# Masked attention over a sparse graph: q rows fetched two tiles ahead, attention started one stage earlier, two loads of W_v issued one stage earlier

## The chip, the cores and the metric

The kernel runs on one core of one Trainium2 chip. The metric is the device time of one execution in microseconds (us). The time before is the median of three runs, 630.4 us (630.32 to 631.99). All arithmetic is in 32-bit floats.

## The reference

One transformer-like layer on a graph of 2708 nodes with 1024 features. `adj` is a 0/1 matrix with about four ones in a row (probability 0.0014771 an entry), so that only a few scores of a row count; the rest is masked with -10000.

```python
h = relu(layernorm(x))                       # x: (2708, 1024)
q, k, v = h @ W_q.T + b_q, h @ W_k.T + b_k, h @ W_v.T + b_v
z = (q @ k.T) / 32                           # scale 1/sqrt(1024)
z = where(z * adj == 0, -10000, z * adj)
x = x + relu(softmax(z, axis=1) @ v)
```

## The kernel before, in words

**What is multiplied.** The kernel first forms M = W_q^T W_k on TensorE, so that a row of "q" is h M plus a bias and a score is the dot product of such a row with a row of h. Nobody forms k. Nor is v formed for all nodes: the weighted sums u of rows of h are multiplied with W_v at the end. Nodes are sorted by their number of neighbours and put into 21 full tiles of 128 rows and one small rest; tile t of a half has at most K[t] neighbours in a row: K = 8, 7, 5, 5, 4, 3, 3, 2 for tiles 0 to 7 and 8, 7, 6, 6, 5, 5, 4, 4, 3, 3, 3, 2, 1 for tiles 8 to 20. Entry 21 (`SECOND`) holds the neighbours over eight of the tiles 0 and 8, seven of them. Tile 20 (`BARE`) has no scores to compute.

**Units and stages.** The main loop (line 1233) goes over 20 units. Units 0 to 9 form q for a pair of tiles: (0, 1), (2, 3) up to (18, 19). Units 10 to 19 multiply the sums u of a pair of tiles with W_v, in the pairs of the list `order` (line 989): (6, 5), (4, 3), (2, 0), (20, 7), (17, 13), (18, 12), (19, 11), (15, 10), (14, 1), (16, 9); tile 8 is left over and done alone at the end. "Stage n" is the pass of the loop for unit n. A unit is a product of two 256-row-by-1024 blocks by Strassen's scheme in its Winograd form: seven products of half-size blocks instead of eight. Each product is one call of `add_block`: four matmul calls, which the profile counts as eight matmuls. `multiply` (line 1046) issues for unit n in this order: s2 T1, a12 B21, s4 B22, s3 T2, then by `between` and `opened` the first two products of unit n+1 (a11 B11, and s1 with T0 in a q unit or with `M[:, 0, 1]` in an o unit), and last a22 T3. B11, B12, B21 and B22 are the quarters of the right-hand matrix: `M[:, 0, 0]`, `M[:, 0, 1]`, `M[:, 1, 0]`, `M[:, 1, 1]`; T0 to T3 are differences of them, in `T[:, 0]` to `T[:, 3]` (the same memory as `wlow`). Between those products `after(i)`, i from 0 to 6, emits everything else: "slot (n, i)" is the i-th of stage n.

**The left-hand operands.** They are needed transposed. In a q unit the rows (`qr`) are gathered from `h_dram` by GpSimd (line 1209, issued in stage n for unit n+2) and TensorE transposes them (line 415). In an o unit the rows of a tile t are either "faced" or held. A faced tile's u is copied in quarters by ScalarE (line 944), stored to `u_dram` (line 946) and loaded by four DMAs of SyncE's queue (line 700), after which VectorE can finish the transposition (line 705). A held tile's u stays in SBUF and TensorE transposes it. `sums` decides when a tile's last sum is emitted (line 940): faced if that is in slot 2 of the stage two before its unit or earlier, or if the unit is the last. s1 to s4 are then formed on VectorE (line 722 and 742).

**Attention.** `attention` (line 959) is a generator that is drained in between: for each tile it emits K[t] score steps on VectorE (line 863: one pass over a gathered tile `g` of h rows and the tile `pq` of q rows, summed up into `zall`), the softmax weights (lines 904 to 912, exponential on ScalarE), and K[t] - 1 weighted sums on VectorE (line 923; line 929 for tiles 0 and 8). The rows of h are gathered by GpSimd into eleven slots `g` (line 610), as slots come free; from stage 10 on two more slots lie in the memory of T0. `fetch(t)` asks for a tile's gathers and gets its q rows: by an indirect gather from `q_dram` for tiles under 8 (line 835, `pq<-q_dram,tab`), by a plain DMA on GpSimd's queue from `q_late` for the others (line 833). The tiles `pq` have a tag with two buffers. Tile t+1 is fetched when tile t's scores have been emitted. Each q unit stores its q rows by SyncE's or ScalarE's queue (line 1086) in `c12` or `c21`.

**What sets the order.** VectorE executes in the order in which the program emits (`manual_schedule`), so a step that waits holds up all that was emitted behind it. How many attention steps are emitted in a slot is planned: a score or a sum counts 1.3, the weights 0.6, and `advance(share)` (line 999) emits steps until the slot's share is used up; `share` (line 1241) is 20.9/7, less 2.3/7 for each faced tile of the next unit, and a little different in stages 9, 10 and the last five. Before, `advance` is first called in slot (5, 0). Where a tile must be ready and isn't (lines 1313 and 1332), steps are emitted beyond the share. SyncE's queue takes its DMAs one after the other: a DMA that waits for a semaphore holds up those behind it.

**W_v.** The four quarters of W_v replace those of M at the change from q to o units (stages 7 to 10; `last_q` is 9). Lines 1268 to 1271 load them on SyncE's queue: W_v's B11 into `M[:, 0, 1]` in stage 7, where it becomes the difference B12 - B11, then in slot (9, 0) B22 into `T[:, 0]` and B11 into `M[:, 0, 0]`, and in slot (9, 3) B21. VectorE forms T1, T2 and T3 from them at slots (9, 3), (10, 0) and (10, 1) (line 1282), and ScalarE copies B22 to its place in slot (9, 4) (line 1274). The last products of a q unit that read `M[:, 0, 0]` and `T[:, 0]` are the two that `opened(9)` issues in stage 8; the first that reads W_v's B11 is that of `opened(10)` in stage 9.

**The end.** The lone tile 8 has its own last products (lines 1382 to 1392): its rows are transposed by VectorE into `T_alone` (line 1329) and TensorE takes them after the last s3 T2.

Of the kernel before, what the change touches and what calls it, by code (L numbers as in the profile page):

```python
# [29 lines left out]
EARLY = 8  # L30
BARE = 20
# [34 lines left out]
def tile_preln_masked_attention(  # L66
# [12 lines left out]
    nc = tc.nc  # L79
# [14 lines left out]
    SECOND = NT - 1  # L94
# [81 lines left out]
    t = 0  # L176
    while t < NT:
# [4 lines left out]
        t = e  # L182
# [17 lines left out]
    M = core.tile([P, 2, 2, 4, NB], FT, name="M")  # L200
# [232 lines left out]
    T = wlow.rearrange("p (k a) (b w) -> p k (a b) w", a=2, b=2)  # L433
# [12 lines left out]
    with tc.tile_pool(name="w", bufs=1, side="left") as wp:  # L446
# [4 lines left out]
        for o in range(DC):  # L451
            nc.sync.dma_start(wq_sb[o], wq_rows[o * P:(o + 1) * P, :])
            part = slice(0, NB) if o == 0 else slice(0, D)
# [4 lines left out]
        t1 = [work.tile([P, D], FT, tag="hT", name=f"t1_{k}", bufs=2) for k in range(2)]  # L458
# [40 lines left out]
        part = stat.tile([P, 3], FT, tag="part", name="part", bufs=1)  # L499
# [107 lines left out]
    def gather(dst, src, t, w, n, skip=False):  # L607
        off = bass.IndirectOffsetOnAxis(ap=ptab.bitcast(U32)[:n, t, w:w + 1], axis=0)
        if skip:
            return nc.gpsimd.indirect_dma_start(out=dst, out_offset=None, in_=src, in_offset=off,  # L610
                                                bounds_check=N - 1, oob_is_err=False)
        return nc.gpsimd.indirect_dma_start(out=dst, out_offset=None, in_=src, in_offset=off)

    rows_of = {}
    FIRST = EARLY // 2
# [187 lines left out]
    wanted, g_of, tq, first_q = [], {}, {}, []  # L803
# [11 lines left out]
    def ask(t):  # L815

        g_of[t] = []
        wanted.extend((t, s) for s in range(K[t]))

    def fetch(t):  # L820

        if t not in g_of:
            ask(t)
        if t == BARE:
            return
        assert formed.issuperset(range(EARLY) if t < EARLY or t == SECOND else (t,)), t
        tq[t] = work.tile([P, D], FT, tag="hT", name=f"pq_{t}", bufs=2)
        if t == SECOND:
            assert EARLY in formed
            gather(tq[t][:HP], q_dram[:, :], t, SLOTS - WIDE, HP)  # L830
            nc.gpsimd.dma_start(tq[t][HP:], q_late[:HP, :])
        elif t >= EARLY:
            nc.gpsimd.dma_start(tq[t], q_late[(t - EARLY) * P:(t - EARLY + 1) * P, :])
        else:
            got = gather(tq[t], q_dram[:, :], t, SLOTS, P)
            if t == order[0]:
                first_q.append(got)

    def fill():
        while wanted and free:  # L840
            t, s = wanted.pop(0)
            g = free.pop(0)
            if s == K[t]:
                half = slice(HOSTS.index(t) * HP, (HOSTS.index(t) + 1) * HP)
                nc.gpsimd.dma_start(g[:HP], v_dram[half, :])
            else:
                with tc.issue_after(first_q[0].ins) if first_q else nullcontext():
                    gathered.append(gather(g, h_dram[:, :], t, s, P, skip=True))
            g_of[t].append(g)

    def chained(step):

        with tc.issue_after(chain[-1].ins):
            chain.append(step())

    def scores(t, then):
        k = K[t]
        for s in range(k if t != BARE else 0):  # L860
            fill()
            junk = work.tile([P, D], mybir.dt.uint8, tag="junk", name="junk2", bufs=1)
            chained(lambda: nc.vector.scalar_tensor_tensor(  # L863
                junk, g_of[t][s], 1.0, tq[t], op0=ALU.mult, op1=ALU.mult, accum_out=zall[:, t, s:s + 1]))
            yield 1.3
        tq.pop(t, None)
        if then is not None:
            fetch(then)
        fill()
        w = stat.tile([P, SLOTS + 1], FT, tag="w", name=f"w_{t}")  # L870
        if t not in EMPTY:
            nc.scalar.activation(w[:, :k], zall[:, t, 0:k], AF.Exp)
        ws[t] = w
# [79 lines left out]
    def marked(lo, hi):  # L953

        with tc.issue_after(chain[-1].ins):
            nc.vector.tensor_scalar(valid[:, lo:hi], ptab.bitcast(U32)[:, lo:hi, 0:SLOTS], float(N) - 0.5, NONE,
                                    op0=ALU.is_lt, op1=ALU.max)

    def attention(order):
        for t in order[:2]:  # L960
            ask(t)
        free.extend(slots)

        fetch(order[0])
        fill()
        yield 0.0
        marked(0, EARLY)
        yield 0.0
        after = order[1:] + [None, None]
        yield from scores(order[0], after[0])  # L970
        for i, t in enumerate(order):
            nxt = after[i]
            ahead = nxt is not None and K[t] + K[nxt] <= HIGH + 1
            part = scores(nxt, after[i + 1]) if nxt is not None else iter(())
            if ahead:

                for _ in range(min(2, K[nxt] - 1)):
                    yield next(part, 0.0)
            weights(t)
            yield 0.6  # L980
            if ahead:
                yield from part
            yield from sums(t)
            yield from part

    done, held, ws, us = set(), {}, {}, {}
    formed = set()
    faced_tiles, whole_second = set(), []
    order = [6, 5, 4, 3, 2, 0, 20, 7, 17, 13, 18, 12, 19, 11, 15, 10, 14, 1, 16, 9, 8]
    assert sorted(order) == list(range(FULL))  # L990
    chain = placed
    stream = attention(order[:order.index(0)] + [SECOND] + order[order.index(0):])
# [6 lines left out]
    def advance(us):  # L999

        spent[0] -= us
        while spent[0] < 0:
            step = next(stream, None)
            if step is None:
                break
            spent[0] += step

    def add_block(bank, a, b, last=True):
        for c in range(4):
            mm = nc.tensor.matmul(bank, a[:, c, :], b[:, c, :], start=False, stop=(c == 3), skip_group_check=True)  # L1010
        return mm
# [3 lines left out]
    def opened(n):  # L1015

        if n not in banks_of:
            return
        X, Z = banks_of[n]
        ops = ops_of[n][0]  # L1020
        add_block(X, ops["a11"], M[:, 0, 0])
        Y = psum.tile([P, NB], FT, tag="acc", name="psy")
        nc.scalar.copy(Y, X)
        if n == FIRST:
            follow("o0")
        products.append(add_block(Z, ops["s1"], T[:, 0] if units[n][0] == "q" else M[:, 0, 1]))
        p5 = small("p5")
        nc.scalar.copy(p5, Z)
        opened_of[n] = Y, p5

    def between(n):

        if n == len(units) - 1:
            single["first"] = one_started(single["banks"], single["turned"][:, 0:4, :])
        else:
            opened(n + 1)

    def one_started(banks, a):

# [150 lines left out]
    def of_wv(i, j):  # L1190

        return wv[j][:, i * 4:(i + 1) * 4, :]
# [26 lines left out]
    last_q = len(q_pairs) - 1  # L1219
# [13 lines left out]
    for n, unit in enumerate(units):  # L1233
# [7 lines left out]
        share = (20.9 if n < len(units) - 5 else 21.5) / 7  # L1241
        if n in (last_q, last_q + 1):
            share -= 2.3 / 7 * (n - last_q + 1)
        nxt = units[n + 1] if n + 1 < len(units) else None
# [4 lines left out]
        def after(i):  # L1249
# [15 lines left out]
                    with tc.issue_after(sorted_at[-1].ins):  # L1265
                        nc.vector.memset(g, 0.0)
            b11, t1, b21, b22 = M[:, 0, 0], M[:, 0, 1], M[:, 1, 0], M[:, 1, 1]
            for at, place, src in (((-2, 0), t1, of_wv(0, 0)), ((0, 0), T[:, 0], of_wv(1, 1)), ((0, 0), b11, of_wv(0, 0)),
                                   ((0, 3), b21, of_wv(1, 0))):
                if (n - last_q, i) == at:  # L1270
                    nc.sync.dma_start(place, src)
            if (n - last_q, i) == (0, 4):
# [21 lines left out]
                nc.vector.tensor_scalar(msq, msq, MLIMIT, None, op0=ALU.is_gt)  # L1294
            if n > FIRST:
                advance(share)
            if nxt is not None:

                if i == (3 if n == 0 else 4 if turn else 0):
                    ops_of[n + 1] = blocks(*rows_of[n + 1], nc.gpsimd if n + 1 < FIRST - 1 else None)  # L1300
                    with tc.issue_after(products[-1].ins) if n + 1 == FIRST else nullcontext():
                        ops_of[n + 1][1]()
                if i == (4 if n == 0 else 5 if turn else 2):
                    ops_of[n + 1][2]()
                    rows_of.pop(n + 1)
                    if n == last_q - 1:
                        all_rows()
                if i == 3:
                    banks_of[n + 1] = banks_for(bp_sb)
                if i == 6 and n + 2 < FIRST:  # L1310
                    natural_rows(n + 2)
                if i == (2 if FIRST <= n <= last_q - 2 else 3 if n == last_q else 4) and n + 2 > FIRST and n + 2 < len(units) and n + 2 not in rows_of:
                    while units[n + 2][0] == "o" and not done.issuperset(units[n + 2][1:]):
                        advance(1.0)
                    rows_of[n + 2] = load_rows(units[n + 2])
# [259 lines left out]
```

## Time and profile before

| what | us |
|---|---|
| median of three timed runs | 630.4 |
| profiled execution, its own time | 635.63 |
| span of the profiled execution, first to last instruction | 633.9 |
| TensorE busy (1579 matmuls) | 623.0 (98%) |
| VectorE busy | 525.2 (83%) |
| GpSimd busy | 370.7 (58%) |
| ScalarE busy | 291.6 (46%) |
| chain that ended last, share on TensorE | 96% |
| mean granted TensorE clock | 0.994 |

In the profile PE is TensorE's matmuls, PEld its weight loads, DVE VectorE, ACT ScalarE, POOL GpSimd and SP SyncE; "SPq" and "POOLq" are the queues of their sequencers. A line of the timeline gives the start and the duration in us, the engine, the line of the kernel, the operation, the tiles it writes and reads (`out<-in`, buffer numbers left out), the number of merged instructions, and in brackets the idle time of the engine before it with what ended it. `ps`, `psy` are the banks of a unit's products, `a`, `s` its left-hand operands, `M` and `wlow` the right-hand ones, `pt` a bank for transposes, `qr` rows for a q unit, `or` rows for an o unit, `pq` q rows of attention, `g` rows of h.

### The profile page before, as it was taken

Reading aid. Unit: us, or ns where it says so; the run is one execution under the profiler, and the core shown is the slowest. Engines: PE = TensorE matmul, PEld = TensorE weight load, DVE = VectorE, ACT = ScalarE, POOL = GpSimd, SP = SyncE. Lnnn points to the kernel's source line nnn. Section 1 sums busy time; section 2 is a strip of 40 time slices with the busy share of each in tenths; the row PEclk is TensorE's granted clock in tenths of the full one; section 3 lists DMA queues with packets and bytes.
Section 4 is the critical chain, followed back from the end, with each engine's and each line's share of the span. In section 5 each row is a group of like instructions: output and inputs, shape, how many; then the busy total and the mean of one; then the engine's idle time right before and its main releaser. Section 6 shows DMA issues by size and latency. Waiting matters only on the chain.

```text
span 633.9 us, 6066 instructions
## 1 busy us (share of the span) xinstructions
PE 623.0 (98%) x1579; PEld 312.0 (49%) x1579; DVE 525.2 (83%) x1022; ACT 291.6 (46%) x421; POOL 370.7 (58%) x394
## 2 busy tenths in 40 slices
PE   9999999999998999999999989999999999999996
PEld 5777766444444544444444434444444444444442
DVE  5999879898897845899897879998988998988741
ACT  3538985749477372443332333444433324342300
POOL 2639960885766677666543432878566776762241
PEclk9999999999999999999999989999999999999999
DMA  8999997598788469996686999899999999996391
GB/s 333 407 365 316 340 351 301 207 320 307 262 257 337 135 196 369 296 410 191 207 343 197 362 346 305 261 335 318 330 285 344 291 297 307 341 286 172 102 295 71
DMA packets 65089, 182.19 MB, mean 287 GB/s; under 512 B 9960, under 2 KB 20024, under 8 KB 64409
## 3 DMA queue, kind: packets, MB, share of 16 engines
q0 software_dynamic: 26656, 86.02, 43.3%
q1 hardware_dynamic: 31594, 71.53, 32.7%
q10 hardware_dynamic: 6798, 24.20, 9.8%
q8 instruction: 14, 0.23, 0.2%
q14 instruction: 27, 0.21, 0.1%
HBM read 146.70 MB, written 43.36 MB: 300 GB/s over the span
## 4 chain that ended last, share of the span: by engine, by line
PE 96%; DMA 3%; issue 0%; POOL 0%; SPq 0%; DVE 0%; ACT 0%; POOLq 0%
PE ps L1010 44%; PE psy L1010 32%; PE ps_y L476 6%; PE ps_x L476 4%; PE ps_z L476 4%; PE pt L415 3%; DMA M<-in_wv_dram 2%; DMA qr<-h_dram,tab 1%; PE ps_y L511 1%; PE ps_h L1226 0%; PE ps_v L594 0%; DVE y_alone L1391 0%; POOL out_dram L1375 0%; ACT q L1101 0%; POOLq L1397 0%
## 5 line engine op out<-in xcount | busy, mean ns | idle before, releaser
L610 POOL DMA_INDIRECT g<-h_dram,tab x93 | 120.5, 1296 | 62.7 <-ACT u L912 21.7
L1010 PE MATMUL ps<-M,a 128*128 128x512 f32 x320 | 145.8, 599 | 2.0 <-DMA M<-in_wv_dram 2.0
L1010 PE MATMUL psy<-wlow,s 128*128 128x512 f32 x320 | 145.1, 596 | 0.0
L863 DVE SCALAR_TENSOR_TENSOR junk<-g,pq 128x1024 uint8<-128x1024 f32 x92 | 112.4, 1221 | 11.8 <-issue 4.9
L1010 PE MATMUL ps<-M,s 128*128 128x512 f32 x240 | 107.9, 592 | 0.0
L1010 PEld LDWEIGHTS ps<-M,a 128*128 128x128 f32 x320 | 60.4, 192 | 75.4 <-issue 71.2
L1010 PEld LDWEIGHTS psy<-wlow,s 128*128 128x128 f32 x320 | 60.6, 192 | 72.9 <-issue 71.9
L923 DVE SCALAR_TENSOR_TENSOR u<-g,coef,u 128x1024 f32<-128x1024 f32 x70 | 89.7, 1281 | 5.5 <-ACT u L912 4.0
L389 DVE FIND_INDEX8 at<-ones,adj 128x8 uint32<-128x685 f32 (+1 forms) x88 | 74.5, 865 | 0.0
L1010 PEld LDWEIGHTS ps<-M,s 128*128 128x128 f32 x240 | 45.5, 190 | 57.2 <-issue 56.5
L1010 PE MATMUL psy<-wlow,a 128*128 128x512 f32 x160 | 71.9, 592 | 0.0
L368 ACT ACTIVATE sized<-adj 128x2708 uint8<-128x2708 f32 (+1 forms) x22 | 54.2, 2465 | 7.9 <-DMA adj<-in_adj_dram 6.6
L1111 POOL DMA_INDIRECT y<-in_x_dram,tab x19 | 34.6, 1821 | 35.6 <-ACT y L1128 24.2
L298 POOL TENSOR_TENSOR hsum<-hsum,x 128x256 f32<-128x256 f32 (+1 forms) x56 | 38.8, 738 | 25.5 <-DVE wlow L444 21.4
L1010 PEld LDWEIGHTS psy<-wlow,a 128*128 128x128 f32 x160 | 30.4, 190 | 38.3 <-issue 37.1
L808 POOL DMA_INDIRECT out_dram<-y,tab x21 | 27.0, 1287 | 19.2 <-issue 13.1
L1010 PE MATMUL ps<-wlow,s 128*128 128x512 f32 x80 | 36.0, 593 | 0.0
L944 ACT COPY v<-u 128x1024 f32<-128x1024 f32 x19 | 19.8, 1044 | 29.1 <-DVE u L923 25.8
L760 ACT COPY ps<-bp_sb 128x512 f32<-128x512 f32 x42 | 24.6, 595 | 10.3 <-DVE y L1146 9.7
L626 POOL DMA_INDIRECT tab_dram<-tab,pos_i x22 | 21.7, 985 | 11.2 <-DVE pos_i L689 5.7
L276 ACT ACTIVATE x<-x,r 128x1024 f32<-128x1024 f32 (+1 forms) x22 | 25.8, 1232 | 5.2 <-POOL r L266 5.2
L912 ACT ACTIVATE u<-g,coef 128x1024 f32<-128x1024 f32 x16 | 18.4, 1149 | 21.3 <-DVE coef L911 13.2
(253 smaller groups left out, 843.4 us busy)
## 6 DMA issues: line engine op xcount, KB each, us to landing
adj<-in_adj_dram SPq DMA_DIRECT2D x21, 1354.0 KB
x<-in_x_dram SPq DMA_DIRECT2D x21, 512.0 KB
h_dram<-x ACTq DMA_DIRECT2D x21, 512.0 KB
u_dram<-v ACTq DMA_DIRECT2D x19, 512.0 KB
or<-u_dram SPq DMA_DIRECT2D x76, 128.0 KB
q_late<-q SPq DMA_DIRECT2D x12, 512.0 KB
pq<-q_late POOLq DMA_DIRECT2D x12, 512.0 KB
M<-in_wv_dram SPq DMA_DIRECT2D x3, 1024.0 KB
```

The lines of the kernel that those rows point to most:

```text
L276: nc.scalar.activation(xs[i][:n], xs[i][:n], AF.Relu, bias=r[:n, 4, i:i + 1], scale=r[:n, 3, i:i + 1])
L298: small.append(nc.gpsimd.tensor_add(hsum[:n, cols], hsum[:n, cols], xt[:n, cols]))
L368: nc.scalar.activation(sized[:n], a[:n, :, :PW], AF.Abs, accum_out=total[:n, t:t + 1])
L389: nc.vector.max_index(at[:n, k - first_k, g, :], ones[:n, 0:8], a[:n, g, :])
L476: mm = nc.tensor.matmul(bank, a_tile(o + H * a[0], a[1], i), b(o), start=first and o == 0, stop=(o == H - 1), skip_group_check=True)
L610: return nc.gpsimd.indirect_dma_start(out=dst, out_offset=None, in_=src, in_offset=off, bounds_check=N - 1, oob_is_err=False)
L760: nc.scalar.copy(return_[h], row[:, h * NB:(h + 1) * NB])
L808: to = nc.gpsimd.indirect_dma_start(out=out, out_offset=bass.IndirectOffsetOnAxis(ap=ptab.bitcast(U32)[:n, t, SLOTS:SLOTS + 1], axis=0), i ...
L863: chained(lambda: nc.vector.scalar_tensor_tensor(junk, g_of[t][s], 1.0, tq[t], op0=ALU.mult, op1=ALU.mult, accum_out=zall[:, t, s:s + 1]))
L923: chained(lambda: nc.vector.scalar_tensor_tensor(u, g_of[t][s], coef[:, s:s + 1], u, op0=ALU.mult, op1=ALU.add))
L1010: mm = nc.tensor.matmul(bank, a[:, c, :], b[:, c, :], start=False, stop=(c == 3), skip_group_check=True)
L1111: return nc.gpsimd.indirect_dma_start(out=y[:n], out_offset=None, in_=x, in_offset=off, compute_op=ALU.add)
```

## The change

Five things, in one edit:

- `fetch` no longer asks for a tile's gathers; that is done when the tile before it has been scored, as before. The q rows of tile t+2 (not t+1) are fetched when tile t's scores have been emitted; a tile whose q isn't formed yet is put on a list, `awaited`, and fetched at the first later score step where it is.
- The q rows of the first two tiles (6 and 5) are fetched at the start.
- `advance(2 * share)` is called in slot (4, 6), so that attention's first steps are emitted there.
- Tile 13 stands ahead of tile 17 in `order`, and so in attention and in unit 14.
- The loads of W_v's B22 (`T[:, 0]`) and B11 (`M[:, 0, 0]`) are emitted in `between` of stage 8, right behind `opened(9)`, instead of in slot (9, 0).

```diff
+    awaited = []
+
+    def is_formed(t):
+        return t == BARE or formed.issuperset(range(EARLY) if t < EARLY or t == SECOND else (t,))
+
+    def fetch_formed():
+        while awaited and is_formed(awaited[0]):
+            fetch(awaited.pop(0))
+
     def fetch(t):
-        if t not in g_of:
-            ask(t)
         if t == BARE:
             return
...
-    def scores(t, then):
+    def scores(t, then, later):
         k = K[t]
         for s in range(k if t != BARE else 0):
+            fetch_formed()
             fill()
...
         tq.pop(t, None)
-        if then is not None:
-            fetch(then)
+        if then is not None and then not in g_of:
+            ask(then)
+        if later is not None:
+            awaited.append(later)
+        fetch_formed()
         fill()
...
         fetch(order[0])
+        fetch(order[1])
         fill()
...
-    order = [6, 5, 4, 3, 2, 0, 20, 7, 17, 13, 18, 12, 19, 11, 15, 10, 14, 1, 16, 9, 8]
+    order = [6, 5, 4, 3, 2, 0, 20, 7, 13, 17, 18, 12, 19, 11, 15, 10, 14, 1, 16, 9, 8]
...
         else:
             opened(n + 1)
+        if n == last_q - 1:
+            nc.sync.dma_start(T[:, 0], of_wv(1, 1))
+            nc.sync.dma_start(M[:, 0, 0], of_wv(0, 0))
...
-            for at, place, src in (((-2, 0), t1, of_wv(0, 0)), ((0, 0), T[:, 0], of_wv(1, 1)), ((0, 0), b11, of_wv(0, 0)),
-                                   ((0, 3), b21, of_wv(1, 0))):
+            for at, place, src in (((-2, 0), t1, of_wv(0, 0)), ((0, 3), b21, of_wv(1, 0))):
...
             if n > FIRST:
                 advance(share)
+            elif (n, i) == (FIRST, 6):
+                advance(2 * share)
```

More of the change, by code (lines that the diff above doesn't have):

```diff
@@ L818, in ask @@
         wanted.extend((t, s) for s in range(K[t]))
+    awaited = []
[4 more added lines that the diff above has]
+            fetch(awaited.pop(0))
     def fetch(t):
-        if t not in g_of:
-            ask(t)
         if t == BARE:
             return
-        assert formed.issuperset(range(EARLY) if t < EARLY or t == SECOND else (t,)), t
+        assert is_formed(t), t
         tq[t] = work.tile([P, D], FT, tag="hT", name=f"pq_{t}", bufs=2)
@@ L968, in attention @@
         yield 0.0
-        after = order[1:] + [None, None]
-        yield from scores(order[0], after[0])
+        after = order[1:] + [None, None, None]
+        yield from scores(order[0], *after[:2])
         for i, t in enumerate(order):
@@ L973, in attention @@
             ahead = nxt is not None and K[t] + K[nxt] <= HIGH + 1
-            part = scores(nxt, after[i + 1]) if nxt is not None else iter(())
+            part = scores(nxt, *after[i + 1:i + 3]) if nxt is not None else iter(())
             if ahead:
```

## The prediction

> **What bounds the kernel now.** I read the page's first part, then TensorE's waits, then TensorE's timeline around those waits, then the queues that feed it.
>
> ```profile
> PE 623.0 (98%) x1579; PEld 312.0 (49%) x1579; DVE 525.2 (83%) x1022; ACT 291.6 (46%) x421; POOL 370.7 (58%) x394
> ```
>
> ```profile
> core 0 of [0], span 633.9 us
> engine line waited for: us in total, times, longest us
> PE pt L415 <- DMA qr<-h_dram,tab: 2.1, 1, 2.1
> PE ps L1010 <- DMA M<-in_wv_dram: 2.0, 1, 2.0
> ```
>
> TensorE is the bound, and in the whole span it waits for a transfer only twice. So the change can gain only by ending such a wait or by taking matmuls away, and can lose only by making TensorE wait somewhere new. The two waits in TensorE's timeline (start, duration, last bracket the idle time before):
>
> ```profile
> 202.98 1.54 PE L415 MATMUL pt<-ident,qr 128*128 128x128 f32 x8 [2.08 <-DMA qr<-h_dram,tab]
> 204.32 4.85 PE L1010 MATMUL psy<-wlow,s 128*128 128x512 f32 x8
> 209.01 1.04 PE L415 MATMUL pt<-ident,qr 128*128 128x128 f32 x8
> ```
>
> ```profile
> 347.57 3.60 PE L1010 MATMUL psy<-wlow,a 128*128 128x512 f32 x8
> ...
> 361.30 3.60 PE L1010 MATMUL psy<-wlow,s 128*128 128x512 f32 x8
> 366.93 5.37 PE L1010 MATMUL ps<-M,a 128*128 128x512 f32 x8 [2.03 <-DMA M<-in_wv_dram]
> 372.13 3.60 PE L1010 MATMUL ps<-M,s 128*128 128x512 f32 x8
> ```
>
> A block (x8, four calls of `add_block`) starts 3.43 us after the one before it: from 347.57 to 361.30 are four blocks in 13.73. At the second wait the start-to-start times are 5.63 and 5.20, so 2.20 us were waited and 1.77 us more were lost in the block behind it: 3.97 us in all. The first wait, by the same reading, cost 2.08, then 4.69 - 3.43 = 1.26 in its block and, with eight transposes at 0.87 (the row at 526.79 below), 1.34 - 0.87 = 0.47: 3.8 us. The windows view says what the extra time is (columns: stretch, its length, then busy time of PE, PEld, DVE, ACT, POOL, then the granted clock, the DMA share and GB/s):
>
> ```profile
> 366.90:372.10 5.20, 5.17 (x8) 2.21 (x9) 2.25 (x3) 0.00 (x0) 3.37 (x3) 0.67 1.03 353
> ```
>
> The clock granted behind the wait was 0.67. 5.20 x 0.67 = 3.5, the normal block: the extra is the clock, and it goes with the wait.
>
> **W_v's loads (a gain).** The wait ends with B11 (`M[:, 0, 0]`, 1 MB). The load queue of SyncE in order of time:
>
> ```profile
> 351.81 0.34 SPq L1086 DMA_DIRECT2D q_late<-q  x1
> 352.25 0.38 SPq L1271 DMA_DIRECT2D wlow<-in_wv_dram  x1
> 352.95 5.44 SPq L1271 DMA_DIRECT2D M<-in_wv_dram  x2
> ```
>
> Both loads stood behind the store of q tile 17, which waits for stage 8's last copy. Their places are free earlier: the last matmul that reads `T[:, 0]` for unit 9 is the block in front of 347.57. Issued there, the two loads leave at about 347.8 and 348.5, 4.5 us sooner. B11 would land at 366.8 - 4.5 = 362.3; TensorE wants it at 361.30 + 3.43 = 364.73. That leaves 2.4 us. Is there room on the DMA engines? What the queues moved in 347.8 to 352.3, and then in 352.3 to 366.8 (packets, MB, share of 16 engines; q1 is SyncE's, q0 GpSimd's):
>
> ```profile
> q0 software_dynamic: 364, 1.30, 89.2%
> ```
>
> ```profile
> q1 hardware_dynamic: 484, 3.05, 50.0%
> q0 software_dynamic: 711, 2.10, 40.5%
> ```
>
> In the first stretch SyncE's queue was empty and the neighbour gathers had the engines. In the second, with both full, SyncE's queue got half of them. If half is what it gets from 347.8 on, the loads keep their pace and, with q 17's 0.5 MB no longer in front, beat 362.3. If the gathers kept their 89% until 352.3, the loads would gain only the store's place: 0.5 MB at 3.05 MB in 14.5 us is 2.5 us, landing at 364.3, still before 364.73 by a hair. The first row pair is the nearer case (two full queues), so I take the whole wait as gone: -3.97. Bound on the other side: no gain, if the loads stay put. A gain above 3.97 is excluded, as no other wait hangs on these loads.
>
> TensorE wants B22's product `T[:, 1]` only at stage 10; VectorE's subtraction for it waited too (row 364.17 below) and comes earlier with T0.
>
> **Eight transposes go (a gain).** The planner charges 1.3 for a score or sum, 0.6 for weights, and hands out `share` = 20.9/7 = 2.99 a slot. `advance(2 * share)` at (4, 6) emits 5.97 worth: all three scores of tile 6 and two of tile 5, five steps that stood in slots (5, 0) and (5, 1). From there every tile's last sum falls about two slots earlier. Counting it through: tile 10's last sum moves from (15, 3) to (15, 1). Tile 10 belongs to unit 17, and `sums` turns its rows on the way through DRAM if it ends by (15, 2); otherwise TensorE transposes them. Before, these are the eight in stage 16:
>
> ```profile
> 261.79 6.87 PE ps L1010 x16
> ...
> 526.79 0.87 PE pt L415 x8
> ```
>
> After, they are gone (-0.87); tile 1 keeps its eight, its slot (16, 4) is the same. VectorE gets two half-tile transposes instead (a whole tile is 1.25 us, row 609.07 below), and a store and four loads of 0.5 MB each way are added, issued a stage ahead of their use. The profiled sum is -3.97 - 0.87 = -4.84 us.
>
> **Steps moved into stage 4 (no cost on TensorE).** VectorE runs them in program order, ahead of unit 6's sums s1 to s4:
>
> ```profile
> 247.62 1.23 DVE L863 SCALAR_TENSOR_TENSOR junk<-g,pq 128x1024 uint8<-128x1024 f32 x1 [4.71 <-issue]
> ...
> 255.02 1.28 DVE L722 TENSOR_TENSOR s<-a,pt 128x512 f32<-128x512 f32 x2 [1.79 <-ACT a L718]
> ```
>
> ```profile
> 239.96 1.04 POOL L612 DMA_INDIRECT pq<-q_dram,tab  x1 [0.30 <-issue]
> ```
>
> The 4.71 idle is tile 5's first score; its q rows were asked of GpSimd at 239.96 only, behind six neighbour gathers. Now they are second in that queue, so this idle goes, and the gathers behind start one issue (1.04 + 0.30) later. A score is 1.25 with the short read behind it (1.23 in the row), so unit 6's s1 is then at 255.0 + 5 x 1.25 - 4.71 - 1.79 + 1.34 = 256.1. TensorE takes it in the second half of the row at 261.79, at 265.2: 7.8 us of cover after the 1.28 of the operation. Were the cover gone, each us of lateness is a us of TensorE, plus the clock.
>
> **Rows of q two tiles ahead; 13 before 17.** The fetch for tile t+2 writes the buffer of tile t, so GpSimd waits for t's last score; behind it in GpSimd's queue stand t+1's neighbour gathers and the row gathers of units 7 to 9. The kernel has such waits already, at the same points:
>
> ```profile
> POOL pq L612 <- DVE junk L863: 8.9, 5, 4.4
> ```
>
> so I cost this at nothing (tile 13 ahead of 17 swaps the same operations); the rows of a unit are gathered nearly two stages (a stage is over 24 us) before use. On VectorE a wait goes: tile 17's first score.
>
> ```profile
> 364.17 2.29 DVE L1282 TENSOR_TENSOR wlow<-wlow,M 128x2048 f32<-128x2048 f32 x1 [1.71 <-DMA wlow<-in_wv_dram]
> ...
> 371.21 1.23 DVE L863 SCALAR_TENSOR_TENSOR junk<-g,pq 128x1024 uint8<-128x1024 f32 x1 [2.95 <-DMA pq<-q_late]
> ```
>
> 1.71 + 2.95 = 4.66 us of idle VectorE lie just where TensorE gains 3.97, so VectorE keeps up.
>
> **What is late next: the end.** With TensorE 4.84 us earlier, the lone last tile decides:
>
> ```profile
> 534.58 0.69 DVE L1127 TENSOR_TENSOR u<-ps,u 128x512 f32<-128x512 f32 x1 [0.57 <-PE ps L1010]
> ...
> 590.95 0.68 DVE L1127 TENSOR_TENSOR u<-ps,u 128x512 f32<-128x512 f32 x1
> ...
> 609.07 1.25 DVE L705 STREAM_TRANSPOSE T_alone<-or 128x1024 f32<-128x1024 f32 x1 [10.76 <-DMA or<-u_dram]
> ```
>
> ```profile
> 610.78 3.60 PE L1010 MATMUL ps<-M,T_alone 128*128 128x512 f32 x8
> ```
>
> Its turned rows are ready at 610.3, half a us before TensorE takes them. At 534.58 VectorE still waits for TensorE; in stage 18 it is late: the bank of 590.95 was ready eight blocks before 610.78, at 583.3. By the planner's count four sums are forced in at (16, 4) before (tile 1 was not done) and none after. A sum is
>
> ```profile
> L923 DVE SCALAR_TENSOR_TENSOR u<-g,coef,u 128x1024 f32<-128x1024 f32 x70 | 89.7, 1281 | 5.5 <-ACT u L912 4.0
> ```
>
> 1.28 us, so 5.1 us of VectorE leave this stretch, and the lone tile comes 5.1 us earlier for a TensorE that comes 4.84 earlier: the half us stays. Without this cover the end would give back up to 4.3 us.
>
> **Against the timed runs.** The profiled execution took 635.63 (span 633.9 and 1.73 around it), 5.23 over the median of 630.4. TensorE's blocks cost the same in both; only waits and the two ends can be shorter. If all 5.23 came out of the two waits' 7.8 us, 2.6 are left, and of W_v's 3.97 about 1.3; if none did, 3.97. I take the middle, 2.65, and with 0.87 the gain is 3.5: **626.9 us**, bounds 625.5 and 628.2. Under 0.3% (1.9 us) a change can't be told from none here.
>
> **Rivals.** (1) *The wait is mostly the profiler's, or the loads stay behind the store.* The order of SyncE's queue is fixed at compile time, and the trace of before can't show the new one. For it: 5.23 us must come from somewhere. Then the transposes and at most 0.9 more are gained: 628.6 to 629.5.
>
> (2) *q 17 comes late (slower).* Its store now stands behind 2 MB of W_v. The Trainium skill's "DMA: Bandwidth & Descriptors", section "Queues, rings and completion order", says the same against this change: within a ring descriptors are consumed in order, and the engines go round between the queues by packet; the half and half above agrees with the latter. By rows: B11 lands at 362.3, the store takes 7.94 as before (351.81 to the fetch that waited for it):
>
> ```profile
> 359.75 1.15 POOL L833 DMA_DIRECT2D pq<-q_late  x2 [4.02 <-DMA q_late<-q]
> ```
>
> and the fetch 11.46 (to 371.21): tile 17 could start at 381.7 at worst. Behind its first score VectorE has, up to unit 11's s1, two subtractions (2.29 each), three scores and two sums (6.3), four half-tile transposes (2.5) and s1 (0.64): 14.0. TensorE wants s1 seven blocks after 372.13, at 396.1 - 4.0 = 392.1. So it decides from 378.1 on; at 381.7 it costs 3.6 and 1.8 of clock: 626.9 + 5.4 = 632.3. Against it: the store's 7.94 and the fetch's 11.46 were measured beside W_v, which would be over by then.
>
> (3) *The slow block is not the wait's.* The Trainium skill's "TensorE: Matmul & The Clock Gate", section "Part 1: The HAM clock gate", lets the clock fall after an idle window of about 3.4 us; by it a wait of 2.03 us need not lower it, and removing the wait would leave the 1.77. Only the 2.20 and 0.87 would go in the profile, 1.5 (the middle, 2.65 x 2.20 / 3.97) and 0.87 in timed runs: 628.0. The trace speaks against it: both waits are near 2 us and a slow block stands right behind each.
>
> **Chances.** Forecast 0.62, rival 1 0.20, rival 2 0.12, rival 3 0.06. Faster by over 0.3%: 0.60 of the forecast, rival 3, and 0.03 of rival 1: 0.69. Within 0.3%: the rest of rival 1, 0.04 of rival 2 and 0.02 of the forecast: 0.23. Slower: 0.08. The range, 625.2 to 629.8, holds the forecast with 0.3 us to spare on the fast side and rival 1; it leaves out rival 2.
>
> **What would show it.** Right: no TensorE wait for `in_wv_dram`, the loads ahead of q 17's store in SyncE's queue and landed before TensorE's use, no granted clock below 1 near 365; eight `pt` transposes less (1571 matmuls), none in stage 16; VectorE without the idle before tile 5's scores; the lone tile turned well before TensorE's use; the first wait unchanged. Wrong: a TensorE wait in stage 10 for VectorE behind a score of tile 17, a wait at the lone tile, or a profiled gain of 4.8 us that the timed runs don't show.

## The result, and the profile after

Medians of the timed runs: 634.07 us after (633.64 to 635.14, 5 runs) and 631.17 before on the same chip (630.32 to 631.99, 5 runs); the ratio is 1.0056, 95% interval 1.0044 to 1.0067. The change made the kernel slower, where 626.9 us, 0.9944 of the 630.4, was forecast. A second comparison of the same two kernels gave 1.0019 (0.9997 to 1.0041), which reaches no change: the loss is small and clear of noise in the first only, but in both the forecast gain is not there.

The profiled execution took 633.64 us, span 631.9. Its busy times, and TensorE's waits:

```profile
PE 621.3 (98%) x1571; PEld 311.4 (49%) x1571; DVE 526.3 (83%) x1024; ACT 291.4 (46%) x421; POOL 363.2 (57%) x394
```

```profile
engine line waited for: us in total, times, longest us
PE psy L1024 <- DVE q L1110: 3.5, 1, 3.5
```

Eight matmuls are gone (1571), and so are both waits of before. One new wait stands there, for VectorE's line 1110, `c22`. TensorE's timeline around it, then VectorE's and GpSimd's:

```profile
283.39 3.60 PE L1024 MATMUL ps<-M,a 128*128 128x512 f32 x8
286.82 3.60 PE L1024 MATMUL ps<-wlow,s 128*128 128x512 f32 x8
293.97 6.46 PE L1024 MATMUL psy<-wlow,a 128*128 128x512 f32 x8 [3.55 <-DVE q L1110]
300.27 1.04 PE L415 MATMUL pt<-ident,qr 128*128 128x128 f32 x8
```

```profile
277.88 1.23 DVE L873 SCALAR_TENSOR_TENSOR junk<-g,pq 128x1024 uint8<-128x1024 f32 x1 [3.70 <-DMA g<-h_dram,tab]
...
282.69 1.23 DVE L873 SCALAR_TENSOR_TENSOR junk<-g,pq 128x1024 uint8<-128x1024 f32 x1 [3.58 <-DMA g<-h_dram,tab]
...
283.84 1.28 DVE L722 TENSOR_TENSOR s<-a,pt 128x512 f32<-128x512 f32 x2
...
293.23 0.68 DVE L1110 TENSOR_TENSOR q<-psy,p 128x512 f32<-128x512 f32 x1
```

```profile
262.24 1.04 POOL L1294 DMA_DIRECT2D M<-in_wv_dram  x1
265.11 1.93 POOL L610 DMA_INDIRECT g<-h_dram,tab  x1 [1.84 <-ACT u L925]
...
270.27 1.88 POOL L610 DMA_INDIRECT g<-h_dram,tab  x1 [0.30 <-DVE u L936]
```

I read these views from the last one up. The transfer at 262.24 adds W_v's B12 (1 MB) onto `M[:, 0, 1]`; the program emits it in slot (7, 6), the scheduler issued it in stage 5. The two neighbour gathers shown behind it are those for tile 2's third and fourth scores (slot (6, 2)). The scores start at 277.88 and 282.69, 12.8 and 12.4 us after their gathers were issued, and VectorE idles 3.70 and 3.58 us for them. Behind them on VectorE stand s1 to s4 of unit 7 (line 722), then c12 (line 1113) and c22 (line 1110) of unit 6. Until c22 has read bank `psy`, TensorE may not write unit 6's last product, a22 T3, into it. A block follows the one before by 3.43 us, so 293.97 - 286.82 - 3.43 = 3.72 us were waited, and 300.27 - 293.97 - 3.43 = 2.87 more lost in the block behind: 6.6 us. The windows view gives that block's granted clock, 0.55 (column PEclk, ahead of the DMA share and GB/s):

```profile
core 0: us, PE busy (x) PEld busy (x) DVE busy (x) ACT busy (x) POOL busy (x), PEclk, DMA share, GB/s
293.90:300.20 6.30, 6.23 (x8) 2.67 (x9) 6.13 (x14) 2.69 (x4) 4.46 (x4) 0.55 0.55 174
```

What was forecast for W_v did happen. SyncE's queue (the scheduler put B11 ahead of B22), and tile 17's first score:

```profile
346.89 0.33 SPq L1053 DMA_DIRECT2D M<-in_wv_dram  x1
350.32 0.33 SPq L1052 DMA_DIRECT2D wlow<-in_wv_dram  x1
354.87 0.33 SPq L1103 DMA_DIRECT2D q_late<-q  x1
```

```profile
373.08 1.23 DVE L873 SCALAR_TENSOR_TENSOR junk<-g,pq 128x1024 uint8<-128x1024 f32 x1 [0.49 <-DMA pq<-q_late]
```

The first wait needs care. Before, unit 4's rows (`qr`) came late; here they were in time:

```profile
197.24 3.60 PE L1024 MATMUL ps<-M,s 128*128 128x512 f32 x8
200.68 1.04 PE L415 MATMUL pt<-ident,qr 128*128 128x128 f32 x8
201.55 3.60 PE L1024 MATMUL psy<-wlow,s 128*128 128x512 f32 x8
204.99 1.04 PE L415 MATMUL pt<-ident,qr 128*128 128x128 f32 x8
```

From the first of these rows to the last it is 7.75 us. Nothing in the change touches that gather, and a second profile of the same kernel has the wait again (1.43 us). It varies from one execution to the next. So I take it out: the time from the block in front of it to the second transposes behind it, less 7.75, is its cost with its slow clock. (Before: 197.30 to 209.01, 3.96; the prediction's 3.8 left out 0.15 of idle time that the bracket doesn't count.) What is left of each span:

| kernel | ratio to before, 95% interval | span | first wait | rest |
|---|---|---|---|---|
| before | 1 | 633.9 | 4.0 | 629.9 |
| after | 1.0056 (1.0044 to 1.0067) | 631.9 | 0 | 631.9 |
| after, again | 1.0019 (0.9997 to 1.0041) | 632.6 | 1.6 | 631.0 |
| W_v's loads only | 1.0089 (1.0059 to 1.0118) | 635.6 | 1.7 | 633.9 |
| W_v's loads and 13 ahead of 17 | 0.9954 (0.9933 to 0.9974) | 627.6 | 1.7 | 625.9 |
| after without the early steps | 0.9955 (0.9939 to 0.9972) | 629.7 | 3.9 | 625.8 |
| after with one share early | 0.9935 (0.9909 to 0.9961) | 627.8 | 1.9 | 625.9 |
| after, accumulating transfer held back | 0.9947 (0.9926 to 0.9969) | 629.3 | 4.2 | 625.1 |
| both of these | 0.9938 (0.9918 to 0.9957) | 627.4 | 1.7 | 625.7 |
| after, rows one tile ahead | 1.0030 (1.0007 to 1.0053) | 634.8 | 4.1 | 630.7 |
| early steps only | 1.0258 (1.0230 to 1.0285) | 648.1 | 1.9 | 646.2 |

(Each ratio is to runs of the kernel before on the same chip. The two kernels with one share came to this stretch 0.5 us later for reasons that lie ahead of it; their rest is that much high.)

### The profile page after: what moved, and what is told of

Its sections match the earlier page's. It is cut to its first block, busy times and chain, and to the rows that moved or that the text cites. A ratio compares the mean times of both kernels' runs of the same rounds, so it can differ in the third digit from the quotient of the medians.

```text
span 631.9 us, 6071 instructions
## 1 busy us (share of the span) xinstructions
PE 621.3 (98%) x1571; PEld 311.4 (49%) x1571; DVE 526.3 (83%) x1024; ACT 291.4 (46%) x421; POOL 363.2 (57%) x394
## 4 chain that ended last, share of the span: by engine, by line
PE 84%; DVE 5%; DMA 4%; issue 4%; POOL 3%; ACT 0%; SPq 0%; POOLq 0%; DVEq 0%
PE ps L1024 38%; PE psy L1024 28%; PE ps_y L476 7%; PE ps_x L476 4%; PE ps_z L476 4%; DMA g<-h_dram,tab 2%; PE pt L415 2%; POOL g L610 1%; DVE s L722 1%; POOL tab_dram L626 1%; DMA pq<-q_dram,tab 1%; DMA M<-in_wv_dram 1%; PE ps_y L511 1%; DVE junk L873 1%; DVE u L936 1%
## 5 line engine op out<-in xcount | busy, mean ns | idle before, releaser
L610 POOL DMA_INDIRECT g<-h_dram,tab x93 | 116.1, 1249 | 51.8 <-issue 19.5
L1024 PE MATMUL ps<-M,a 128*128 128x512 f32 x320 | 144.0, 593 | 0.0
L936 DVE SCALAR_TENSOR_TENSOR u<-g,coef,u 128x1024 f32<-128x1024 f32 x68 | 87.2, 1283 | 5.8 <-ACT u L925 4.0
L1024 PE MATMUL psy<-wlow,a 128*128 128x512 f32 x160 | 74.8, 612 | 3.5 <-DVE q L1110 3.5
L925 ACT ACTIVATE u<-g,coef 128x1024 f32<-128x1024 f32 x18 | 20.7, 1149 | 18.9 <-DVE coef L924 14.4
L626 POOL DMA_INDIRECT tab_dram<-tab,pos_i x22 | 21.6, 982 | 13.2 <-DVE pos_i L689 7.7
```

Of the source, the lines that this page charges most:

```text
L626: put = nc.gpsimd.indirect_dma_start(out=tab_dram[lo >= EARLY][:, :], out_offset=bass.IndirectOffsetOnAxis(ap=pos_i[:n, t:t + 1], axis=0), ...
L936: chained(lambda: nc.vector.scalar_tensor_tensor(u, g_of[t][s], coef[:, s:s + 1], u, op0=ALU.mult, op1=ALU.add))
```

## The experiments

My theory A: the gathers behind the accumulating transfer land late, the early steps let VectorE run onto them, and c22 stands behind them. B: the moved steps as such are too much for VectorE. C: rows fetched two tiles ahead stand in front of tile 2's gathers.

**W_v's loads alone** (on the kernel before):

```diff
+        if n == last_q - 1:
+            nc.sync.dma_start(T[:, 0], of_wv(1, 1))
+            nc.sync.dma_start(M[:, 0, 0], of_wv(0, 0))
...
-            for at, place, src in (((-2, 0), t1, of_wv(0, 0)), ((0, 0), T[:, 0], of_wv(1, 1)), ((0, 0), b11, of_wv(0, 0)),
-                                   ((0, 3), b21, of_wv(1, 0))):
+            for at, place, src in (((-2, 0), t1, of_wv(0, 0)), ((0, 3), b21, of_wv(1, 0))):
```

> The kernel before with one part of the change alone: the loads of W_v's B22 and B11 are emitted in stage 8, behind opened(9). Theory A and B alike (the wait for B11 is in the timed runs of before, and the loss of the change lies elsewhere): TensorE's wait for in_wv_dram and the slow block behind it go, 3.97 us in before's profile, so about 627.2 us beside a before of 631.2. Rival (the wait for B11 is mostly the profiled execution's own): no change, 630 to 631.

637.48 us, slower by 0.9%, which no theory had expected. SyncE's queue, VectorE and TensorE of its profile:

```profile
345.65 0.35 SPq L1038 DMA_DIRECT2D wlow<-in_wv_dram  x1
346.05 0.43 SPq L1039 DMA_DIRECT2D M<-in_wv_dram  x1
349.70 0.33 SPq L1089 DMA_DIRECT2D q_late<-q  x1
```

```profile
372.25 1.23 DVE L863 SCALAR_TENSOR_TENSOR junk<-g,pq 128x1024 uint8<-128x1024 f32 x1 [7.91 <-DMA pq<-q_late]
...
374.67 0.68 DVE L1096 TENSOR_TENSOR q<-psy,p 128x512 f32<-128x512 f32 x1
```

```profile
366.05 3.60 PE L1010 MATMUL ps<-M,s 128*128 128x512 f32 x8
375.41 5.18 PE L1010 MATMUL psy<-wlow,a 128*128 128x512 f32 x8 [5.76 <-DVE q L1096]
380.43 3.60 PE L1010 MATMUL psy<-wlow,s 128*128 128x512 f32 x8
```

The W_v wait is gone, and VectorE idles 7.91 us at tile 17's first score, for q 17's rows. Behind that score stand another and c22 (in this kernel line 1096), for which TensorE waits: 5.93 and 1.59 in the block behind it, 7.5 us. The rest of the kernel without this wait is 633.9 - 7.5 = 626.4.

The prediction's second rival, a store held up by the loads in front of it, is only a part of this. The score starts at 372.25, against 371.21 before. From the store of q 17 to the score it is 372.25 - 349.70 = 22.55 us, against 19.40 before, so by estimate the loads ahead of it took 3.15. The other part is the gain itself. Before, c22 stood behind the same score, and TensorE's next block came just late enough:

```profile
373.63 0.69 DVE L1093 TENSOR_TENSOR q<-psy,p 128x512 f32<-128x512 f32 x1
```

c22 ended at 374.32 and its block began 3.43 us after 372.13, at 375.56: 1.25 us of cover. With TensorE 3.97 us sooner and the rows no later, 2.7 us would have been waited here; with the rows 3.15 later as well, my estimate is 3.97 + 3.15 - 1.25 = 5.9.

**The change without its early steps, and with one share of them:**

```diff
-            elif (n, i) == (FIRST, 6):
-                advance(2 * share)
```

```diff
-                advance(2 * share)
+                advance(share)
```

> The changed kernel without advance(2 * share) in slot (4, 6): attention's first steps are emitted from (5, 0) on, as before; all else as changed. Theory A (gathers behind the accumulating 1 MB DMA of GpSimd's queue land late, and the moved steps let VectorE run onto them ahead of unit 7's operations) and theory B (it is the moved steps as such): TensorE's wait for VectorE's L1110 in stage 6 goes, tile 10 is held again (+0.87): about 627.2 us. Theory C (the q rows fetched two tiles ahead stand in front of tile 2's gathers and make them late): the wait in stage 6 stays, at least 629.5 us.

> The changed kernel with advance(share) in place of advance(2 * share) in slot (4, 6): three scores moved instead of five; tile 10 is still faced, by the planner's count. Theory A: where the accumulating DMA comes in GpSimd's queue against the gathers decides, so anything from no wait in stage 6 (626.4 us) to the whole of it (633 us). Theory B: two steps (2.5 us) less in front of unit 7's operations, so the wait of 3.7 us shrinks to about 1.2, with 1 to 3 us of slow clock: 628.5 to 630.5 us.

630.26 and 629.39 us: both faster than before, and in neither is there a stage-6 wait. With one share, VectorE meets tile 2's third and fourth scores only behind s1 to s4:

```profile
279.79 1.29 DVE L722 TENSOR_TENSOR s<-a,pt 128x512 f32<-128x512 f32 x2 [0.17 <-ACT a L718]
...
284.76 1.22 DVE L873 SCALAR_TENSOR_TENSOR junk<-g,pq 128x1024 uint8<-128x1024 f32 x1 [0.67 <-DMA g<-h_dram,tab]
...
290.25 0.68 DVE L1110 TENSOR_TENSOR q<-psy,p 128x512 f32<-128x512 f32 x1
```

**The accumulating transfer held back**, all else as in the change:

```diff
-                nc.gpsimd.dma_start(t1, of_wv(0, 1), accum_op=ALU.add)
+                with tc.issue_after(gathered[-1].ins):
+                    nc.gpsimd.dma_start(t1, of_wv(0, 1), accum_op=ALU.add)
```

> The changed kernel with one edit: the accumulating DMA of W_v (B12 added into M[:, 0, 1], 1 MB, GpSimd's queue) is issued behind the last neighbour gather emitted by slot (7, 6), where the program emits it; in the changed kernel it stands two stages earlier in GpSimd's queue, ahead of tile 2's gathers. Theory A: tile 2's gathers land about 5 us after their issue instead of 12, VectorE's two waits of 3.70 and 3.58 us and TensorE's wait in stage 6 go: about 626.4 us, faster than both kernels. Theory B and C: the waits in stage 6 stay, about 633 us.

629.23 us, and no stage-6 wait with all the early steps in place. The transfer now leaves at 317.80. GpSimd, VectorE and TensorE:

```profile
268.03 1.87 POOL L610 DMA_INDIRECT g<-h_dram,tab  x1 [2.87 <-ACT u L925]
...
273.19 1.89 POOL L610 DMA_INDIRECT g<-h_dram,tab  x1 [0.30 <-DVE u L936]
...
317.80 1.03 POOL L1295 DMA_DIRECT2D M<-in_wv_dram  x1
```

```profile
281.85 1.23 DVE L873 SCALAR_TENSOR_TENSOR junk<-g,pq 128x1024 uint8<-128x1024 f32 x1 [3.60 <-DMA g<-h_dram,tab]
...
292.38 0.68 DVE L1110 TENSOR_TENSOR q<-psy,p 128x512 f32<-128x512 f32 x1
```

```profile
294.35 3.60 PE L1024 MATMUL psy<-wlow,a 128*128 128x512 f32 x8
```

The gather for the fourth score is used 8.7 us after its issue, not 12.4, and the third score doesn't wait at all. I had expected 5 us and neither of VectorE's waits; the one for the fourth score stays, at 3.60. c22 ends at 293.06, 1.3 us ahead of its block: little cover, but enough. This profile has a first wait of 4.2 us, so TensorE comes to stage 6 4.1 us later than in the profile of the change, and a part of the cover may be owed to that. The fair neighbour is the kernel with rows one tile ahead (below), whose first wait is 4.1: its block is due at the same time (294.40, against 294.35), its transfer still leaves ahead of the gathers, at 267.03, and TensorE waits. This speaks for A and against B. It does not separate the place in the queue from the load on the DMA engines, since the transfer moved in both.

**The change again**, beside the next two, with no edit.

> The changed kernel again, profiled a second time beside the three kernels of this call. In its first profile the wait for the rows of unit 4 (qr, 2.08 us and slow clock before the change) was missing and one wait of 3.5 us for VectorE's c22 in stage 6 stood there. If that stage-6 wait belongs to the kernel: again 3 to 4 us at the same block, whether or not the first wait is there, and ratio to before 1.003 to 1.008. If the two exclude each other by chance of one execution: no stage-6 wait when the first wait is there, and a ratio below 1.0 in at least some rounds.

The stage-6 wait was there again at 3.73 us (3.90 and 1.80 by starts, 5.7 us), beside a first wait of 1.43; the two don't exclude each other. The ratio, 1.0019, is below what I expected, with an interval that reaches into it.

**Both cures:** one share, and the transfer held back.

> The change with one share instead of two at the last slot of stage 4, and the accumulating W_v transfer held behind the gather issued last before it in program order. Theory A (the gathers behind that transfer land late, and VectorE reaches them ahead of stage 6's c12 and c22): each of the two edits alone has already ended the stage-6 wait, so both together bring nothing more: 0.993 to 0.995 of before, within 0.3% of each alone. If the two cures were independent gains of their own: 0.988 to 0.990.

0.9938, no more than either alone: they end the same wait. c22 has more room here; it ends at 287.41 and its block starts at 292.48.

**W_v's loads and tile 13 ahead of 17** (on the kernel before):

```diff
-    order = [6, 5, 4, 3, 2, 0, 20, 7, 17, 13, 18, 12, 19, 11, 15, 10, 14, 1, 16, 9, 8]
+    order = [6, 5, 4, 3, 2, 0, 20, 7, 13, 17, 18, 12, 19, 11, 15, 10, 14, 1, 16, 9, 8]
```

with the edit of the first experiment.

> The kernel before with W_v's B22 and B11 loaded sooner and tile 13 ahead of 17, nothing else. The W_v move alone gave 1.009 of before with a wait of 5.8 us in stage 9 for VectorE's c12. Theory S (q 17's store, now behind 2 MB of W_v, brings tile 17's rows late, and its first score holds VectorE ahead of c12): with 13's scores first, no stage-9 wait and the W_v wait gone: 0.993 to 0.996 of before. Rival T (2 MB issued sooner slow all gathers of stages 8 and 9): a stage-9 wait of at least 2 us stays, 1.000 to 1.009.

0.9954: theory S. (What the expectation calls c12 is c22, at line 1096 of this kernel; it is the one on `psy`.) At the place where VectorE stood 7.91 us it now goes through tile 13's scores without a stop:

```profile
363.46 0.68 DVE L1099 TENSOR_TENSOR q<-ps,u 128x512 f32<-128x512 f32 x1
364.06 1.22 DVE L863 SCALAR_TENSOR_TENSOR junk<-g,pq 128x1024 uint8<-128x1024 f32 x1
...
366.47 0.69 DVE L1096 TENSOR_TENSOR q<-psy,p 128x512 f32<-128x512 f32 x1
```

The rest falls from 633.9 to 625.9: the swap is worth 8.0 us beside the sooner loads.

**Rows of q one tile ahead**, all else as in the change; VectorE's order is the same:

```diff
-        fetch(order[1])
...
-        yield from scores(order[0], *after[:2])
+        yield from scores(order[0], after[0], after[0])
...
-            part = scores(nxt, *after[i + 1:i + 3]) if nxt is not None else iter(())
+            part = scores(nxt, after[i + 1], after[i + 1]) if nxt is not None else iter(())
```

> The change whole, but rows of q fetched one tile ahead as before; VectorE's order is the same, in GpSimd's queue each fetch of rows stands later, the accumulating transfer still ahead of tile 2's last gathers. Theory A: the stage-6 wait stays at 2 to 4 us, and VectorE waits in stage 4 for tile 5's rows as before: 1.002 to 1.008 of before. Theory C (the rows fetched two ahead stand in front of tile 2's gathers and are what delays them): no stage-6 wait, 0.993 to 0.997.

The stage-6 wait stays, and the whole of it:

```profile
PE psy L1024 <- DVE q L1110: 3.6, 1, 3.6
```

C falls. The rest, 630.7, is 0.3 below that of the change profiled again: fetching two ahead neither caused the loss nor brought a gain that shows.

**The early steps alone** (the kernel before, with the two shares in slot (4, 6) and nothing else):

```diff
             if n > FIRST:
                 advance(share)
+            elif (n, i) == (FIRST, 6):
+                advance(2 * share)
```

> The kernel before with nothing but the two shares of attention's steps handed out at the last slot of stage 4. Theory A (these steps bring VectorE to tile 2's last scores ahead of the gathers behind the accumulating transfer, and stage 6's c22 stands behind them): a stage-6 wait of TensorE for c22 of 3 to 4 us with slow clock behind it, 6.6 us, less 0.87 for eight transposes; the W_v wait of stage 10 may stay: 1.006 to 1.011 of before. Rival (the stage-6 wait needs another part of the change beside it): no stage-6 wait, 0.997 to 1.000.

649.85 us, 2.6% slower: far more than the 1.1% that I expected at most. TensorE's two long waits, and VectorE at the second:

```profile
297.09 5.30 PE L1010 MATMUL psy<-wlow,a 128*128 128x512 f32 x8 [4.37 <-DVE q L1093]
...
383.23 6.58 PE L1010 MATMUL ps<-M,s 128*128 128x512 f32 x8 [10.38 <-DVE s L722]
```

```profile
375.05 1.23 DVE L863 SCALAR_TENSOR_TENSOR junk<-g,pq 128x1024 uint8<-128x1024 f32 x1 [18.24 <-DMA pq<-q_late]
```

The stage-6 wait is there without any other part of the change, as A has it. What I missed is stage 9: VectorE, two shares further on, reaches tile 17's first score while that tile's rows are still on their way, and stands 18.24 us, ahead even of unit 10's left-hand operands. (The store of q 17 left at 357.18; the scheduler had put both W_v loads ahead of it, at 348.85 and 352.28, though the program emits them later.) Tile 13 ahead of 17 covers this as well: in the kernel with rows one tile ahead the loads and the store left at nearly the same times (350.06, 353.49 and 358.30), 13 comes first, and TensorE doesn't wait in stage 9.

## Why the prediction was wrong, point by point

**W_v's loads, -3.97: right in size, but only with the swap beside them.** From before to W_v's loads with the swap the rest falls by 629.9 - 625.9 = 4.0 us, and none of the kernels with sooner loads waits for `in_wv_dram`. That VectorE keeps up because 4.66 us of its idle time lie there was wrong: 2.95 of them were a wait for q 17's rows, which do not come earlier with TensorE, and without the swap c22 stands behind them.

**Eight transposes, -0.87: right.** 1571 matmuls; between the kernel without them and with the stage-6 wait cured (625.1) and two that still have them (the change without early steps, 625.8, and W_v's loads with the swap, 625.9) lie 0.7 and 0.8 us.

**Steps moved into stage 4 (no cost on TensorE): the step that failed.** At unit 6's s1, where I gave them 7.8 us of cover, they did cost nothing. But I followed them no further. From there every step is earlier, also those of stage 6, and their gathers are earlier by less. GpSimd's queue before, and tile 2's third score and c22 on VectorE:

```profile
257.95 1.03 POOL L1278 DMA_DIRECT2D M<-in_wv_dram  x1
...
272.85 0.99 POOL L610 DMA_INDIRECT g<-h_dram,tab  x1 [1.02 <-ACT u L912]
...
277.69 1.92 POOL L610 DMA_INDIRECT g<-h_dram,tab  x1 [1.92 <-DVE u L923]
```

```profile
286.13 1.22 DVE L863 SCALAR_TENSOR_TENSOR junk<-g,pq 128x1024 uint8<-128x1024 f32 x1
...
288.55 0.69 DVE L1093 TENSOR_TENSOR q<-psy,p 128x512 f32<-128x512 f32 x1
```

The gathers for tile 2's third and fourth scores went out 7.7 and 7.4 us earlier in the change (265.11 and 270.27), but VectorE was free for the third score 12 us earlier (277.88 less 3.70 of idle time, 274.18). A part of all three is the first wait, missing in this profile; in the kernel with rows one tile ahead, which has it, they are 2.9, 3.2 and 7.1 us. And the accumulating transfer, which stood 15 and 20 us ahead of these gathers before, stands 3 and 8 us ahead of them in the change. That the scheduler issues it in stage 5 is in the trace of before, at 257.95; the prediction doesn't mention it. I also took s1 for VectorE's only deadline. There is another: c22 has to read its bank before the unit's last product may be written. Before, it ended at 289.24, 5.0 us ahead of that block (294.28). With 625.1 as the rest without it, 6.6 more gives 631.7 (631.9 was measured), and 5.7 gives 630.8 for the second profile (631.0). Both gains and this one loss account for the result.

**13 ahead of 17, costed at nothing: right for the operations it swaps, wrong for what it hides.** It is what makes both the sooner loads and the early steps bearable: 8.0 us beside the loads, and the wait of 10.4 us, with its slow clock, beside the steps. Rows two tiles ahead were rightly costed at nothing.

**What is late next: the end.** No kernel waits there. The change has its lone tile turned 4.2 us ahead of use, where I had half a us:

```profile
603.05 1.25 DVE L705 STREAM_TRANSPOSE T_alone<-or 128x1024 f32<-128x1024 f32 x1 [10.42 <-DMA or<-u_dram]
```

```profile
608.50 3.60 PE L1024 MATMUL ps<-M,T_alone 128*128 128x512 f32 x8
```

TensorE comes only 2.28 earlier than before (610.78), not 4.84, and the lone tile 6.02. That the end would give back up to 4.3 without its cover isn't borne out: with W_v's loads and the swap alone the sums forced in at (16, 4) stay by the planner's count, and that kernel lost nothing there (turned at 603.33, used at 604.49).

**Against the timed runs.** Of the 5.23 us between profile and median up to 4.0 can be the first wait, which comes and goes and which the change doesn't touch; where the other 1.3 lie is open. Whether W_v's wait had a share, as my middle of 2.65 out of 3.97 assumed, isn't decided: timed, the loads with the swap gain 0.46%, 2.9 us (1.7 to 4.2), which holds both 2.65 and 3.97. Without its new wait the change gives 0.9935 to 0.9947, about the 0.9944 forecast.

**The rivals.** The first is refuted where it has the loads behind the store; its other half, a wait that is mostly the profiler's, allowed 0.9 us, and the timed gain of at least 1.7 speaks against it. The second is a real mechanism, some 3.15 of the 5.93 us waited in the first experiment, but in the change the swap hides it; and its bound was wrong in the same way as my own step: I let it decide from 378.1, by s1, while a score that starts at 372.25 already cost 7.5 us, by c22. The third is refuted: where the W_v wait goes, the slow block behind it goes too.

## What to carry over

For each engine that runs in program order, list every reader that frees a bank, not only the writers of operands: work moved ahead of such a reader can be paid for at the next write of that bank. A step moved earlier moves all steps behind it, so ask of each transfer that they wait for whether it is earlier by as much; and where a compile-time scheduler may hoist a large transfer, look where it went. Ending a wait of the engine that bounds can uncover what had its cover from that wait: here c22 of unit 9, with 1.25 us to spare. When a change has several parts, one part may be there to pay for another: the parts alone were 0.9% and 2.6% slower, and W_v's loads with the swap 0.5% faster.

## What the runs showed of the hardware

The edge of the slow clock lies in a narrow place here. Behind the first wait the next block was at full pace after six waits of 1.43 to 1.72 us (granted clock 1.00 in each) and slow after four of 2.01 to 2.33 (0.67 to 0.76). Two of them, W_v's loads with the swap and the transfer held back:

```profile
202.35 1.06 PE L415 MATMUL pt<-ident,qr 128*128 128x128 f32 x8 [1.52 <-DMA qr<-h_dram,tab]
203.25 3.60 PE L1010 MATMUL psy<-wlow,s 128*128 128x512 f32 x8
```

```profile
203.06 1.72 PE L415 MATMUL pt<-ident,qr 128*128 128x128 f32 x8 [2.33 <-DMA qr<-h_dram,tab]
204.58 4.67 PE L1024 MATMUL psy<-wlow,s 128*128 128x512 f32 x8
```

From the wait of 1.72 us to that of 2.01 the cost by the table goes from 1.9 to 3.9 us. The Trainium skill's "TensorE: Matmul & The Clock Gate", section "Part 1: The HAM clock gate", gives an idle window of about 3.4 us; here waits of 2.0 us were enough, and the measurement decides.

Gathers used right when they landed took 12.8 and 12.4 us from issue where the accumulating 1 MB had been issued 3 and 8 us ahead of them, and 8.7 us (one gather) with it moved away. In the DMA view of the change that transfer itself took 13.2 us to land.
